# Fetching the last image's rows inside the loop of a two-layer convolution and state-space kernel

## The chip, the cores and the metric

The kernel runs on one core of a Trainium2 chip. The metric is the device time of one execution in microseconds, as the median of several runs; for the kernel before it is 13595.54 us (three runs, 13595.24 to 13596.91). The engines are called PE (matrix products), ACT (activations), DVE (vector work), POOL (GpSimd) and SP, which does no arithmetic here and issues nearly all transfers between main memory and the on-chip buffers.

## The reference

Eight images of 128 channels by 128 by 128 pass through two layers. The first (a dilated convolution, Fourier transforms and an attention over channels) is not touched. The second is, cut to what matters:

```python
y = conv2d(x, conv_w, 3x3, padding 1) + conv_b
seq = y.reshape(B * H * W, 8, 16)          # 8 tokens of 16 channels in each pixel
xi, z = split(seq @ in_proj)
xc = silu(causal_conv1d(xi)); dt, B, C = split(xc @ x_proj)
dt = softplus(dt * dt_w + dt_b)
for t in range(8):                          # 32 x 16 states in each pixel
    h = exp(dt[t] * A) * h + dt[t] * B[t] * xc[t]
    y[t] = sum(h * C[t])
out = ((y + D * xc) * silu(z)) @ out_proj
g = (out - mean) / sqrt(var + eps)          # in 4 groups of channels, over the whole image
return x + silu(g * gn_w + gn_b)
```

The mean and variance run over an image, so the last line can be computed for an image only when all of its rows are through.

## The kernel before, in words

Layer 2 (`layer1` in the code) cuts each image into 32 blocks of four rows (`RB = 4`), 256 blocks in all, `nb = 256`. All engines follow one order written out by hand: the tuple `ORDER` lists the pieces of work of one turn of the loop, each with a number `ahead`; in turn `i` a piece works on block `i + ahead`. So a turn holds the end of block `i - 1`, the middle of block `i` and the beginning of blocks `i + 1` and `i + 2`. Each engine runs its instructions strictly in this order, and SP issues its transfers in it too.

What the pieces around the change do, with the lines of the profile:

- `exps` (ACT, L851), `decay` (DVE, L870, L873, L875), `inject` (DVE L864, two of 16 on POOL L862), `add` (DVE, L880) and `weigh` (POOL, L886) are the scan over tokens, in 16 steps `s` a block. A step's state lies in a buffer `h` (`hp`, nine of them, 128 x 1024 values of four bytes), its weighted state in a buffer `hc` (`hcp`, nine). `collect` (PE, L987) and `ends_sum` (PE, L952, L957) sum the `hc` into the block's output and so free them. The first two steps of `weigh` in POOL's turn are 8 and 15; `decay` of step 15 multiplies what `weigh` of step 15 made.
- `lay_first` and `lay_ends` (SP, L913 and L905/L906) put rows of two projections into `bcs`; `end_products` (POOL, L935) multiplies them to `cb`, the first thing POOL does in a turn; `lay_cross` (SP, L943) spreads `cb` to `cbx`, which `cross` (DVE, L892) uses.
- `store_inputs` and `lay_inputs` (SP, L824, L831) pass `u` through main memory to `ud` for POOL's `inject`; `lay_states` (SP, L815) spreads the projections to `bb` and `cc`.
- `lay_own` and `lay_own_first` (SP, L924, L930) gather rows of `u` into `us`; `own_terms` (DVE, L964) multiplies them with what `ends_sum` made; `own_add` (PE, L971), `gated` (DVE, L994), `project_out` (PE, L1002), `result` (ACT, L1012) and `spread_of` (ACT, L1020/L1021) follow it, and `keep` (SP, L1025) stores the block's output to `gn` in main memory.
- `norm` calls `norm_of` (L1036 to L1055) when an image's last block is through: from the sums it makes a scale `sc` and an offset `bi`.

The last line of the reference is done for image 0 to 6 inside the loop, one block of rows a turn, while the next image is under way: `last_load` (SP, L1070/L1071, two loads of 256 KB into `v` and `res`, two buffers each), `last_act` (ACT, L1077, a Silu, with a load of ACT's function table before it and one for the exponential after it), `last_sum` (POOL, L1083) and `last_store` (SP, L1089). Since the seventh image's norm comes in turn 226, two of its 32 blocks of rows are left when the loop ends; a small loop does them there.

For the last image nothing is under way any more. Its 128 rows are done in 16 groups of eight rows (`TR = 8`), `k = 0 .. 15`: `tail_load(k)` takes one of the nine `h` and one of the nine `hc` buffers and loads 512 KB of `gn` (SP, L1133) and 512 KB of `x1` (SP, L1134) into them; `tail(k)` does the Silu (ACT, L1139), the sum (DVE, L1140) and the store of 512 KB (SP, L1141). Six groups are loaded ahead (`AHEAD = 6`).

SP has eight semaphores for its transfers and takes them in turn, so a transfer is issued only when the one eight before it has landed.

Of the kernel before, what the change touches and what calls it, by code (L numbers as in the profile page):

```python
# [595 lines left out]
def layer1(ctx, tc, x1, w1, c1, out):  # L596
# [96 lines left out]
    nb = len(blocks)  # L693
# [10 lines left out]
    def live(i):  # L704
        return 0 <= i < nb
# [321 lines left out]
    def norm_of(b):  # L1027

        mv = wk2.tile([P, 2], F32, name="mv")
        gmv = wk2.tile([P, 2], F32, name="gmv")  # L1030
        dv = wk2.tile([P, 1], F32, name="dv")
        sc = wk2.tile([P, 1], F32, name="sc")
        bi = wk2.tile([P, 1], F32, name="bi")
        nr = H // RB
        st, dm = stats[b], wk1.tile([P, nr], F32, name="dm")
        nc.vector.tensor_reduce(mv[:, 0:1], st[:, 0], AX.X, ALU.add)  # L1036
        nc.vector.tensor_scalar(mv[:, 0:1], mv[:, 0:1], 1.0 / HW, None, ALU.mult)
        nc.vector.tensor_scalar(dm, st[:, 0], 1.0 / N, mv[:, 0:1], ALU.mult, ALU.subtract)
        nc.vector.tensor_mul(dm, dm, dm)
        nc.vector.scalar_tensor_tensor(dm, dm, float(N), st[:, 1], ALU.mult, ALU.add)  # L1040
        nc.vector.tensor_reduce(mv[:, 1:2], dm, AX.X, ALU.add)
        nc.vector.tensor_scalar(mv[:, 1:2], mv[:, 1:2], 1.0 / HW, None, ALU.mult)
        ps = misc().rearrange("p a b -> p (a b)")
        nc.tensor.matmul(ps[:, 0:2], cf("group"), mv, start=True, stop=True)
        nc.vector.tensor_copy(gmv, ps[:, 0:2])
        nc.vector.tensor_sub(dv, mv[:, 0:1], gmv[:, 0:1])
        nc.vector.tensor_mul(dv, dv, dv)
        ps = misc().rearrange("p a b -> p (a b)")
        nc.tensor.matmul(ps[:, 0:1], cf("group"), dv, start=True, stop=True)
        nc.vector.tensor_scalar(sc, ps[:, 0:1], gmv[:, 1:2], GN_EPS, ALU.add, ALU.add)  # L1050
        nc.scalar.activation(sc, sc, AF.Sqrt)  # L1051
        nc.vector.reciprocal(sc, sc)  # L1052
        nc.vector.tensor_mul(sc, sc, wf("gn_w"))  # L1053
        nc.vector.tensor_mul(bi, gmv[:, 0:1], sc)  # L1054
        nc.vector.tensor_sub(bi, wf("gn_b"), bi)  # L1055
        tails.extend((b, r, sc, bi) for r in range(0, H, RB))
# [6 lines left out]
    loaded, active, summed = [], [], []  # L1063

    def last_load(i):
        if tails:
            b, r, sc, bi = tails.pop(0)
            v = wk2.tile([P, RB, W], F32, name="v")
            res = wk2.tile([P, RB, W], F32, name="res")
            nc.sync.dma_start(v, gns[b][:, r:r + RB, :])  # L1070
            nc.sync.dma_start(res, x1[b][:, r:r + RB, :])  # L1071
            loaded.append((b, r, sc, bi, v, res))

    def last_act(i):
        if loaded:
            b, r, sc, bi, v, res = loaded.pop(0)
            nc.scalar.activation(v, v, AF.Silu, bias=bi, scale=sc)  # L1077
            active.append((b, r, v, res))

    def last_sum(i):  # L1080
        if active:
            b, r, v, res = active.pop(0)
            nc.gpsimd.tensor_add(res, res, v)  # L1083
            summed.append((b, r, res))

    def last_store(i):
        if summed:
            b, r, res = summed.pop(0)
            nc.sync.dma_start(out[b, :, r:r + RB, :], res)  # L1089
# [38 lines left out]
    def tail_load(k):  # L1128
        if k < len(ends_of):
            b, r = ends_of[k]  # L1130
            v = hp.tile([P, TR, W], F32, name="h")
            res = hcp.tile([P, TR, W], F32, name="hc")
            nc.sync.dma_start(v, gns[b][:, r:r + TR, :])  # L1133
            nc.sync.dma_start(res, x1[b][:, r:r + TR, :])  # L1134
            held[k] = v, res

    def tail(k, sc, bi):
        (b, r), (v, res) = ends_of[k], held.pop(k)
        nc.scalar.activation(v, v, AF.Silu, bias=bi, scale=sc)  # L1139
        nc.vector.tensor_add(res, res, v)  # L1140
        nc.sync.dma_start(out[b, :, r:r + TR, :], res)  # L1141

    AHEAD = 6
    E = mybir.EngineType
    with tc.manual_schedule(engines={E.PE, E.Activation, E.DVE, E.Pool, E.SP}):
        for i in range(-4, nb + 3):
            for f, ahead, *k in ORDER:
                if live(i + ahead) or i + ahead == -1 and f in FIRST:
                    f(i + ahead, *k)
        i = nb  # L1150
        while tails or loaded or active or summed:
            last_load(i)
            last_act(i)
            last_sum(i)
            last_store(i)
        assert not tails
        for k in range(AHEAD):
            tail_load(k)
        b = ends_of[0][0]
        norm_of(b)  # L1160
        _, _, sc, bi = tails[0]
        for k in range(len(ends_of)):
            tail(k, sc, bi)
            tail_load(k + AHEAD)


def network(tc, x, w0, w1, c0, c1, out):
    B = x.shape[0]
    with tc.tile_pool(name="dram", bufs=1, space=DRAM) as dram:
        x1 = [dram.tile([C, H, W], F32, name=f"x1_{b}") for b in range(B)]  # L1170
        layer0(tc, x, w0, c0, x1)
        layer1(tc, x1, w1, c1, out)
# [73 lines left out]
```

## Time and profile before

| what | us |
|---|---|
| median of the runs | 13595.54 |
| profiled execution, its own time | 13597.71 |
| profiled execution, span | 13594.9 |
| busy: PE, DVE, POOL, ACT | 13227.2, 11943.4, 11940.1, 10091.1 |
| one block in the loop | 44.5 |
| end of the last matrix product of `project_out`, from the span's start | 13517.13 |
| first load of the last image's rows | 13529.72 |
| first store of the last image's rows | 13539.48 |

All times of events are counted from the span's start in the one profiled execution. "A <- B" behind an idle time names what ended it. A time of an SP line is that of issuing a transfer, not of its landing; the landing is in a view of its own. Busy times of PE are of pipelined work and say little alone.

### The profile page before, as it was taken

To read this page: it belongs to the slowest core of one execution; us is meant where nothing else is said; L and a number is where in the kernel's file an instruction comes from. 1 tells how busy PE (TensorE), PEld (TensorE's weight loads), DVE (VectorE), ACT (ScalarE), POOL (GpSimd) and SP (SyncE) were. 2 spreads that over 40 slices of the span, in tenths; PEclk is the share of its full clock that TensorE was granted. 3 is DMA by queue.
4 is the path that set the end of the run, shared out by engine and by line. 5 is a ranking of instruction groups with operands and counts; after the bars stand their busy time and mean duration, and the time that the engine had idled before them with its cause. 6 is when DMAs were issued, how large, how long until landed. Compare 5 with 4: busy or idle time off the path is not lost. (4 is left out here: it accounts for less than half of the span.)

```text
span 13594.9 us, 255193 instructions
## 1 busy us (share of the span) xinstructions
PE 13227.2 (97%) x97850; PEld 4812.6 (35%) x97850; DVE 11943.4 (88%) x11710; ACT 10091.1 (74%) x11827; POOL 11940.1 (88%) x6533
## 2 busy tenths in 40 slices
PE   9999999999999999999999999999999999999996
PEld 5676663333333333332333333332333333323332
DVE  3343349999999999999999999999999999999997
ACT  3454367777788878887888878887888788878886
POOL 6766659999899999999999989999999999989996
PEclk9999999999999999999999999999999999999998
DMA  4544455555566666666666666666666666666666
GB/s 132 160 133 125 144 128 135 134 129 135 137 154 149 152 145 153 152 150 147 150 154 150 149 146 151 153 149 148 148 154 152 144 153 150 154 142 154 150 150 177
DMA packets 1183640, 1996.65 MB, mean 147 GB/s; under 512 B 149616, under 2 KB 411824, under 8 KB 1174224
## 3 DMA queue, kind: packets, MB, share of 16 engines
q1 hardware_dynamic: 1181840, 1977.82, 60.0%
q8 instruction: 769, 12.60, 0.4%
q14 instruction: 455, 3.73, 0.1%
q10 hardware_dynamic: 576, 2.50, 0.1%
HBM read 687.75 MB, written 218.10 MB: 67 GB/s over the span
## 5 line engine op out<-in xcount | busy, mean ns | idle before, releaser
L886 POOL TENSOR_TENSOR hc<-h,cc 128x1024 f32<-128x1024 f32 x3584 | 8424.7, 2375 | 308.2 <-PE s L840 219.9
L851 ACT ACTIVATE s<-s 128x1024 f32<-128x1024 f32 x3584 | 3558.2, 1005 | 1185.5 <-PE s L840 1166.7
L840 PE MATMUL s<-dt,m_a 32*128 32x512 f32 x14336 | 3525.2, 638 | 17.0 <-DVE h L880 14.5
L875 DVE TENSOR_TENSOR s<-s,h 128x1024 f32<-128x1024 f32 x2560 | 3134.3, 1224 | 46.0 <-ACT s L851 22.4
L864 DVE TENSOR_TENSOR h<-s,bb 128x1024 f32<-128x1024 f32 x2560 | 3100.6, 1215 | 55.2 <-DMA bb<-all_b 20.2
L880 DVE TENSOR_TENSOR h<-s,h 128x1024 f32<-128x1024 f32 x2560 | 3094.7, 1217 | 54.5 <-DVE s L875 1.8
L840 PE MATMUL s<-u,l_ct 32*128 32x512 f32 x10240 | 2892.2, 641 | 50.2 <-DVE h L873 18.4
L734 PE MATMUL pm<-xin,l_wt 128*32 128x508 f32 (+3 forms) x18432 | 2409.2, 595 | 6.2 <-DVE wk L650 5.5
L987 PE MATMUL yps<-hc,l_ct 128*32 128x512 f32 x14336 | 1889.6, 598 | 61.5 <-ACT yps L980 55.9
L851 ACT ACT_TABLE_LOAD x1247 | 1599.9, 1283 | 235.8 <-DVE h L880 136.6
L840 PEld LDWEIGHTS s<-dt,m_a 32*128 32x128 f32 x14336 | 969.1, 183 | 1275.0 <-DVE h L880 629.7
L840 PEld LDWEIGHTS s<-u,l_ct 32*128 32x128 f32 x10240 | 768.2, 183 | 1438.5 <-DVE h L880 521.2
L862 POOL TENSOR_TENSOR h<-ud,bb 128x1024 f32<-128x1024 f32 x512 | 1220.8, 2384 | 2.4 <-DMA ud<-uw 2.4
L792 POOL TENSOR_TENSOR u<-dt,xc 128x512 f32<-128x512 f32 x512 | 656.0, 1281 | 458.5 <-ACT dt L787 456.6
L734 PEld LDWEIGHTS pm<-xin,l_wt 128*32 128x32 f32 x18432 | 469.3, 109 | 1588.4 <-issue 1586.7
L987 PEld LDWEIGHTS yps<-hc,l_ct 128*32 128x32 f32 x14336 | 394.9, 109 | 1288.8 <-issue 1024.3
L870 DVE TENSOR_TENSOR hc<-s,hc 128x1024 f32<-128x1024 f32 x512 | 623.6, 1218 | 199.4 <-ACT s L851 191.0
L787 ACT ACT_TABLE_LOAD x511 | 655.6, 1283 | 40.9 <-PE pm L782 23.9
L980 ACT ACTIVATE yps<-xc,l_wt 128x512 f32<-128x512 f32 x511 | 352.1, 689 | 403.3 <-DVE ym L994 403.3
L873 DVE TENSOR_TENSOR h<-s,h 128x1024 f32<-128x1024 f32 x512 | 621.5, 1214 | 0.0
L892 DVE TENSOR_TENSOR hc<-s,cbx 128x1024 f32<-128x1024 f32 x512 | 620.4, 1212 | 0.0
L782 PE MATMUL pm<-xc,m_dt 128*32 128x512 f32 x4096 | 545.6, 605 | 1.4 <-ACT yT L752 0.7
(202 smaller groups left out, 15362.6 us busy)
## 6 DMA issues: line engine op xcount, KB each, us to landing
cc<-all_c SPq DMA_DIRECT2D x1792, 256.0 KB, 5.5
bb<-all_b SPq DMA_DIRECT2D x1536, 256.0 KB, 5.7
ud<-uw SPq DMA_DIRECT2D x1024, 256.0 KB, 4.1
xin<-x SPq DMA_DIRECT2D x152, 768.0 KB, 5.1
xin<-x SPq DMA_DIRECT2D x112, 640.0 KB, 6.6
us<-u SPq DMA_DIRECT2D x1025, 64.0 KB, 1.9
cbx<-cb SPq DMA_DIRECT2D x512, 128.0 KB, 2.4
gn<-xr SPq DMA_DIRECT2D x256, 256.0 KB, 2.2
```

Source lines behind the costliest of these rows:

```text
L734: nc.tensor.matmul(d["pm"][c, a:b, wa:wb], convw[:, t, c], xin[:, r + dy + a - lo:r + dy + b - lo, wa + dx:wb + dx], start=(k == 0), stop= ...
L787: nc.scalar.activation(d["dt", hf], flat(d["pm"]), AF.Softplus, bias=wf("dt_b"))
L792: nc.gpsimd.tensor_mul(d["u", hf], d["dt", hf], d["xc"][:, hf, :])
L840: nc.tensor.matmul(d[name, s][:, q], m[a:a + DI, t % LP, :], d[src, t // LP][a:a + DI, :], start=True, stop=True)
L851: nc.scalar.activation(da, da, AF.Exp)
L862: nc.gpsimd.tensor_mul(h, d["ud", t][:, k:k + GP, :], state_row(i, "bb", t))
L864: nc.vector.tensor_mul(h, d["ups", s], state_row(i, "bb", t))
L870: nc.vector.tensor_mul(d["hc", s], da, d["hc", s])
L875: nc.vector.tensor_mul(da, da, d["h", s - GP])
L880: nc.vector.tensor_add(h, d["da", s], h)
L886: nc.gpsimd.tensor_mul(hc, d["h", s if t < L - 1 else s - GP], state_row(i, "cc", t))
L987: nc.tensor.matmul(d["yps"][g * DI:(g + 1) * DI], gather[:, t % LP, :], d["hc", GP * t + g // GP][:, g % GP], start=False, stop=t in LAST, ...
```

## The change

Two things change, both in the part of `layer1` that runs the order.

First, in the last four turns that work on a block `i` (252 to 255), the pieces of the last line are run a second time at the end of the turn: what is loaded, computed or summed is carried through to its store (`last_act`, `last_sum`, `last_store` until nothing is left), and then one more group of rows is loaded with `last_load`. So a turn does two of the seventh image's blocks of rows instead of one. By the end of turn 254 all are loaded, and turn 255 stores the last.

Second, the first loads of the last image are no longer issued after the norm's predecessors at the end, but inside the loop, in turn 256, behind the last piece that takes an `h` or `hc` buffer (that is the `weigh` of step 12 of block 255), and they are nine groups instead of six. The later ones are issued, as before, one after each `tail(k)`, now for group `k + 9`.

```diff
-    AHEAD = 6
+    AHEAD = 9
+    TAKES = (inject, decay, weigh, cross)
+    last_i = nb - 1 - min(ahead for f, ahead, *_ in ORDER if f in TAKES)
+    last_at = max(at for at, (f, ahead, *_) in enumerate(ORDER) if f in TAKES and last_i + ahead == nb - 1)
+    MORE = 4
     E = mybir.EngineType
     with tc.manual_schedule(engines={E.PE, E.Activation, E.DVE, E.Pool, E.SP}):
         for i in range(-4, nb + 3):
-            for f, ahead, *k in ORDER:
+            more = nb - MORE <= i < nb
+            for at, (f, ahead, *k) in enumerate(ORDER):
                 if live(i + ahead) or i + ahead == -1 and f in FIRST:
                     f(i + ahead, *k)
+                if (i, at) == (last_i, last_at):
+                    for k in range(AHEAD):
+                        tail_load(k)
+            if more:
+                while loaded or active or summed:
+                    last_act(i)
+                    last_sum(i)
+                    last_store(i)
+                last_load(i)
         i = nb
         while tails or loaded or active or summed:
             last_load(i)
...
         assert not tails
-        for k in range(AHEAD):
-            tail_load(k)
         b = ends_of[0][0]
         norm_of(b)
```

In the built order `keep` of block 254 and `lay_own_first` of block 255 stand on SP behind the eighteen loads, since they come later in `ORDER`. At the ends of turns 252, 253 and 254 SP has, ahead of the next turn's transfers, two stores (L1089) and two loads (L1070, L1071); POOL has one more L1083 behind its last `weigh` of the turn and ahead of `cb`; ACT has one more L1077 with its table load, and one more table load for L851.

## Prediction

> **What bounds the kernel now.** I read first the busy times by stretch, one block (44.5 us) to a line, then what DVE and POOL waited for, then the timeline of one block boundary, then the timeline of the end with the DMA issues.
>
> ```profile
> 13308.00:13352.50 44.50, 44.20 (x340) 13.74 (x340) 43.33 (x40) 36.20 (x41) 41.84 (x21) 1.00 0.62 145
> 12134.50:12179.00 44.50, 35.39 (x240) 11.16 (x241) 39.26 (x43) 28.16 (x32) 29.52 (x14) 0.85 0.47 119
> 13530.00:13595.00 65.00, 0.00 (x0) 0.00 (x0) 19.82 (x18) 21.11 (x17) 0.00 (x0) 0.50 0.99 391
> ```
>
> ```profile
> DVE hc L870 <- ACT s L851: 178.8, 235, 1.1
> ...
> POOL cb L935 <- DMA bcs<-all_c: 98.2, 91, 2.6
> ```
>
> Columns of the first three: stretch, its length, then PE, PEld, DVE, ACT, POOL, granted clock, DMA share, GB/s. A usual block is bound by DVE: its one regular wait is 0.75 us, before `decay` of step 15 (L870), so whatever stops DVE longer is lost. The second line is a block in which PE sat idle for 8.04 us (an image's norm): the clock fell to 0.85. The third is the end: DMA 0.99, nothing else busy for a third of it. The waits (total us, times, longest) say that POOL's `cb` (L935) is already held at times by rows (`bcs`) that SP lays.
>
> The boundary between blocks 253 and 254 (start, duration, engine):
>
> ```profile
> 13392.99 0.60 SPq L913 DMA_DIRECT2D bcs<-all_b  x1
> 13393.68 0.60 SPq L913 DMA_DIRECT2D bcs<-all_c  x1
> ...
> 13394.74 2.36 POOL L886 TENSOR_TENSOR hc<-h,cc 128x1024 f32<-128x1024 f32 x1 [0.86 <-PE s L840]
> 13397.05 0.74 POOL L935 TENSOR_TENSOR cb<-bcs 128x256 f32<-128x256 f32 x1
> 13397.74 2.37 POOL L886 TENSOR_TENSOR hc<-h,cc 128x1024 f32<-128x1024 f32 x1
> 13400.48 7.00 POOL L886 TENSOR_TENSOR hc<-h,cc 128x1024 f32<-128x1024 f32 x3 [0.37 <-DVE h L873]
> ...
> 13404.01 1.23 DVE L870 TENSOR_TENSOR hc<-s,hc 128x1024 f32<-128x1024 f32 x1 [0.76 <-ACT s L851]
> ```
>
> SP lays `bcs` before POOL has finished the old block; then `cb`, `weigh` 8, `weigh` 15, and L870 takes what `weigh` 15 made.
>
> The end:
>
> ```profile
> 13512.03 0.69 DVE L964 TENSOR_TENSOR own<-pm,us 128x512 f32<-128x512 f32 x1 [5.62 <-PE yps L987]
> ...
> 13529.72 0.42 SPq L1133 DMA_DIRECT2D h<-gn  x1
> 13530.10 0.16 DVE L1055 TENSOR_TENSOR bi<-l_wt,bi 128x1 f32<-128x1 f32 x1
> ...
> 13539.48 0.34 SPq L1141 DMA_DIRECT2D out<-hc  x1
> ```
>
> ```profile
> out<-res SPq DMA_DIRECT2D x2, 256.0 KB, 2.2
> h<-gn SPq DMA_DIRECT2D x16, 512.0 KB, 10.0
> ```
>
> `own_terms` of block 255 (L964) starts the chain to the norm's `bi`; the first of 16 stores leaves at 13539.48, the span ends at 13594.9. A load of 512 KB lands 4.06 us after its issue when first (13529.72, its ACT_TABLE_LOAD starts at 13533.78), 10.0 us in a full queue; there one transfer takes 1.28 us (first ACTIVATEs on new `h` at 13536.89, 13539.45, 13542.03: 2.56 for two).
>
> **What the skill says.** "DMA: Bandwidth & Descriptors", Queues, rings and completion order: SP has one row of rings, and a ring's descriptors are consumed in order. The trace agrees: 512 KB takes 10 us with eight transfers outstanding, about 8 x 1.28. "TensorE: Matmul & The Clock Gate", HAM oscillation: PE gaps over some 3.4 us halve the clock; here 8.04 us did (0.85 over that block). "ScalarE: Activation LUTs", What ACT_TABLE_LOAD costs: 1283 ns and a drain of 1380 ns. The trace shows the 1.28 and no drain (the ACTIVATE follows 0.01 us later); I take 1.28.
>
> **The change, part by part.** The sum is against the profiled execution: span 13594.9, 13597.71 in all, 2.2 over the median.
>
> (a) Second leftover at the ends of blocks 252, 253, 254. ACT gets, after `result` (ends 13396.48), a table load, a Silu and a table load back: 1.28 + 0.81 + 1.28 = 3.37. `exps` 10 then ends at 13400.9 instead of 13397.8; DVE loses 2.85 there. The Silu ends at 13398.6, so POOL's new sum runs 13398.65 to 13399.93. SP waits for it: its new store stands *ahead* of the next block's issues. Behind it wait one `v` and one `res` load, `uw`, both `bcs`, `us`, `cbx`, `ud`, `bb`, `cc`. From 13399.95: store 0.45, `v` 0.6, `res` 0.45, `uw` 0.8, first `bcs` 0.65, so the second is issued at 13402.9 and lands about 2.3 later (the tile's landings: 1.9 least, 2.0 median), 13405.2. Only then runs `cb`: to 13406.0; `weigh` 8 to 13408.3; `weigh` 15 to 13410.65. L870 starts there instead of 13404.01: 6.64 lost, the 2.85 within it. Later users have room: `ud` lands by 13414 for an `inject` at 13423; `bb` by 13417 for DVE at 13422. POOL, 8.0 late, catches up in its 2.7 us of idle time per block. Three boundaries: 19.9. PE sits idle some 4 us at each. Where the norm halved the clock, DVE waited 1.67 and 0.69 more; I take about 1 a boundary (bounds 0 and 2.4): 3. Sum of (a): **+23**.
>
> (b) Leftovers gone from the end. They delayed the square root: `sc` is there at 13521.81, and without them `bi` is done 1.05 later, at 13522.85 instead of 13530.26: **-7.4**.
>
> (c) Nine pairs of loads after the last `weigh` in SP's order. Each waits for its `hc` buffer, freed in PE's order: after `collect` of 8 (13502.3), of 10 (13504.8), of 11 (13509.3), the two `cross` (13510 to 13511), the last four (to 13513.7). Behind all eighteen stand `keep` of block 254 and the last row of `us` (lay_own_first, L930; issued at 13494.75 now), and `own_terms` waits for that row. From the third `hc` on, the bytes queue: first landing 13509.35 + 4.06 = 13513.4, the second 1.75 later as in the present burst, then eleven more at 1.28 to 13529.3; `keep` and `us` 0.9: 13530.2. SP may have eight outstanding, so it can't even issue `us` before the eighth transfer ahead of it has landed (13521.6). `own_terms` starts at 13530.2 instead of 13512.03: +18.2; its chain runs at half clock after that PE gap, +0.9 (16 matmuls of L1002 take 2.00 at full clock): **+19.1**. Bounds: if `us` overtakes the loads in 1.9 us, +11.6; if they are slower, +21.
>
> (d) The tail. From `bi` to the first store 1.28 + 1.24 + 1.22 and gaps = 3.8. Nine tiles lie ready; 16 stores and 7 pairs are left, 30 transfers where 48 were. But with nine buffers, and all nine in use, the `hc` load of tile k+9 waits for store k to *land*, and store k+1 stands behind that load on SP. So seven turns are a chain, not a stream. In a turn the load and the next store are issued within 0.8 us of a landing, the store behind the load. No row shows it. Below: bytes alone, 3 x 1.28 = 3.84. Above: the present burst's pair, second landing 4.06 + 1.76 = 5.8. A 256 KB store alone lands after 2.2 against 2.9 for a load, so a store second comes sooner: I take 5.0. First store landed after 3.0, six turns 30, last load and nine stores 4.06 + 9 x 1.28 = 15.6, end of program 1.6: 50.2. With 3.8: 54.0 from `bi`, where it is 64.6 now (13594.9 - 13530.26): **-10.6** (-19 to -5).
>
> Sum: 23 - 7.4 + 19.1 - 10.6 = **+24.1 us**. On the median, 13595.5 + 24.1 = 13620, slower by 0.18%.
>
> What can be told from no change is put at 0.2%, 27.2 us, so this stands just inside it.
>
> **Rivals.**
> 1. *Slower by more than that.* Same mechanism, with the clock: each PE gap halves it for several windows and DVE waits 2.4 a boundary (+4), a turn costs 5.8 (+5.6): +34, 13629. For: block 254 has no convolutions and shows 2.17 us of such a wait already. Against: at the norm most of the half clock cost nothing. It decides from 3 us above my sum.
> 2. *Not slower.* One mechanism: the boundary stall is absorbed. Stretches 13444 to 13492 and later have DVE at 42.85 of 48.0, so a late start might only fill idle time; (a) falls to 0 and +1 is left, -7 if the turns run at the byte rate: 13588 to 13597. Against: in 252 and 253 DVE has 0.75 us of idle time, and POOL, PE and ACT shift with it. It decides where L870 starts less than 0.5 us late.
> 3. *The row of `us` is not held*, landing 1.9 after issue: (c) falls by 7.5, +17, 13612. Against: the order of the ring.
> 4. *The change does not fetch early*: no. In the built order the loads stand in block 256, ahead of the norm, each waiting for its own buffer alone.
>
> **How the numbers follow.** The forecast, +24 with some 6 us either way, 0.48, of which 0.12 lies over 27.2; rival 1, +27 to +45, 0.30; rival 3, 0.11; rival 2, 0.08; a gain over 27.2, 0.03: (a) at nothing, `us` free and turns at the byte rate together give only 24 - 23 - 7.5 - 8.1 = -15, so it would need something I don't see. Slower 0.12 + 0.30 = 0.42, within 0.2% 0.36 + 0.11 + 0.08 = 0.55, faster 0.03. The likeliest is the sum, 13620. Range: down to rival 3's 13612 with a few us of (d), 13604; up past rival 1, 13636.
>
> **What would show it.** Right: at three boundaries SP's second L1089 after POOL's second L1083, `cb` waiting for `bcs` by 5 us, L870 waiting for POOL about 5 us; L964 waiting 17 us for a DMA of `us` late in the end; PE idle beside a full DMA; in the tail SP's L1134 waiting for `out<-hc`, stores 5 us apart, then 1.28. Wrong: `cb` on time, L964 released by PE, or stores 3.8 apart from the first.

## The result and the profile after

The changed kernel takes 13625.08 us (median of 14 runs, 13621.84 to 13631.74), the kernel before in the same session 13596.2 (14 runs, 13593.6 to 13598.76). The ratio is 1.0021 with a 95% interval of 1.0013 to 1.0029: slower by 28.9 us, where +24.1 was forecast. The profiled span is 13624.4 where it was 13594.9, 29.5 more.

The table divides the 29.5 by stage. A stage ends where one instruction starts in both profiles: `decay` 15 (L870) of each turn, then `own_terms` of block 255 (the last L964), then the norm's `bi` ready (start of the last L1055 plus its 0.16), then the end of the span.

| stage | before, us | after, us | difference | forecast |
|---|---|---|---|---|
| up to L870 of turn 252, ahead of the change | 13315.03 | 13318.28 | +3.3 | 0 |
| L870 of turn 252 to 253 | 44.49 | 50.79 | +6.3 | |
| 253 to 254 | 44.49 | 50.64 | +6.2 | |
| 254 to 255 | 47.0 | 54.34 | +7.3 | |
| 255 to 256 | 48.96 | 47.87 | -1.1 | |
| the four together, (a) | 184.94 | 203.64 | +18.7 | +23 |
| L870 of turn 256 to `own_terms`, (c) | 12.06 | 31.32 | +19.3 | +18.2 |
| `own_terms` to `bi`, (b) and the half clock of (c) | 18.23 | 12.43 | -5.8 | -7.4 + 0.9 |
| `bi` to the end, (d) | 64.64 | 58.73 | -5.9 | -10.6 |

The +3.3 of the first row arises before anything of the change has run. Over the profiles of this study that L870 starts anywhere from 13311.31 to 13322.88, so the row says how far two profiles differ by themselves; the stages below it give +26.3.

The boundary between blocks 253 and 254, POOL's timeline of the kernel after (start, duration, engine; the bracket holds the idle time before and what ended it):

```profile
13404.30 2.36 POOL L886 TENSOR_TENSOR hc<-h,cc 128x1024 f32<-128x1024 f32 x1 [0.90 <-DMA bb<-all_b]
13408.24 1.26 POOL L1083 TENSOR_TENSOR res<-res,v 128x512 f32<-128x512 f32 x1 [1.59 <-ACT v L1077]
13414.33 0.72 POOL L935 TENSOR_TENSOR cb<-bcs 128x256 f32<-128x256 f32 x1 [4.83 <-DMA bcs<-all_c]
13415.01 9.28 POOL L886 TENSOR_TENSOR hc<-h,cc 128x1024 f32<-128x1024 f32 x4
```

SP's timeline of the same boundary, and after it SP's issues at the end of the kernel:

```profile
13399.69 10.18 SPq L1089 DMA_DIRECT2D out<-res  x2
13409.93 0.42 SPq L1070 DMA_DIRECT2D v<-gn  x1
13410.44 0.40 SPq L1071 DMA_DIRECT2D res<-x  x1
13410.90 0.51 SPq L824 DMA_DIRECT2D uw<-u  x1
13411.46 0.61 SPq L913 DMA_DIRECT2D bcs<-all_b  x1
13412.17 0.60 SPq L913 DMA_DIRECT2D bcs<-all_c  x1
...
13516.68 0.54 SPq L1133 DMA_DIRECT2D h<-gn  x1
...
13542.16 0.32 SPq L1134 DMA_DIRECT2D hc<-x  x1
13543.45 0.32 SPq L1025 DMA_DIRECT2D gn<-xr  x1
13544.68 0.51 SPq L930 DMA_DIRECT2D us<-u  x1
```

The first line holds both stores of the turn: SP stands in it for 10.18 us, until POOL's second sum ends at 13409.50. Only then come the five issues down to `bcs`, the last at 13412.17. In POOL's view `cb` waits 4.83 us for it, where it followed its predecessor at once before, and the first two `weigh` behind it (merged into the x4) bring L870 to 13419.71. At the end the same shape returns: `us` (L930) stands behind all eighteen loads, the last issued at 13542.16.

What DVE waited for from 13340 on (total us, times, longest), then PE's timeline at two boundaries:

```profile
DVE hc L1140 <- DMA hc<-x: 26.5, 6, 4.7
DVE own L964 <- DMA us<-u: 25.1, 1, 25.1
DVE hc L870 <- POOL hc L886: 11.3, 4, 4.1
DVE s L875 <- ACT s L851: 10.7, 7, 2.8
```

```profile
13362.13 1.13 PE L840 MATMUL s<-u,l_ct 32*128 32x512 f32 x4 [2.55 <-DVE h L873]
...
13412.93 2.07 PE L840 MATMUL s<-u,l_ct 32*128 32x512 f32 x4 [4.05 <-DVE h L873]
```

The third and fourth waits are for the most part the two halves of a boundary: ACT late by 2.8 us (`exps` behind the Silu and the tables), then POOL late by up to 4.1. In PE's view the same four products take 1.13 us after a gap of 2.55 and 2.07 after 4.05, so the clock is halved at once at the second boundary. At the first it falls too, only a little later. A stretch behind it (columns as in the prediction; the clock is the 0.50):

```profile
13364.00:13367.00 3.00, 3.00 (x16) 0.60 (x16) 0.94 (x1) 2.78 (x4) 3.00 (x3) 0.50 0.47 117
```

At the second boundary the half clock shows from 13412.93 on, less than 7 us before the L870 that ends the step. So what it costs has to be looked for in the next step too: 253 to 254 has a mean clock of 0.93, and 254 to 255, the one of +7.3, has 0.80.

The end, from the chain of waits (start, length, what was waited for or run):

```profile
13533.50 11.17 DMA hc<-x
13544.68 8.43 DMA us<-u
13553.24 0.70 DVE own L964
...
13572.88 6.09 DMA out<-hc
13578.98 0.32 SPq L1134
13579.40 5.39 DMA out<-hc
13584.80 0.32 SPq L1134
13585.22 5.34 DMA out<-hc
```

The eighth semaphore back (a load of `hc`, 11.17 us) holds the issue of `us`; its 64 KB then take 8.43 us to land, where the median landing of that row is 1.9. The tail below is a chain of one thing: a store lands, SP issues the `hc` load that waited for its buffer, and 0.42 us after the landing the next store. One turn is 0.42 + 5.4 = 5.8 us.

Lengths, busy times (PE, PEld, DVE, ACT, POOL), clock, DMA share and GB/s of two stretches of the kernel after:

```profile
13404.00:13455.00 51.00, 41.08 (x236) 12.36 (x239) 40.55 (x38) 35.08 (x39) 39.79 (x20) 0.80 0.55 131
...
13578.00:13624.40 46.40, 0.00 (x0) 0.00 (x0) 9.15 (x8) 7.90 (x7) 0.00 (x0) 0.50 0.84 289
```

The first is the block behind the second boundary: DVE works 40.55 of 51 us where a usual block has 43.3 of 44.5. The second is the tail: the transfers move 289 GB/s, where the kernel before had 391 in its own.

### The profile page after: what moved, and what is told of

Its sections match the earlier page's. It is cut to its first block, busy times and chain, and to the rows that moved or that the text cites. A ratio compares the mean times of both kernels' runs of the same rounds, so it can differ in the third digit from the quotient of the medians.

```text
span 13624.4 us, 255211 instructions
## 1 busy us (share of the span) xinstructions
PE 13235.4 (97%) x97850; PEld 4814.3 (35%) x97850; DVE 11947.4 (88%) x11710; ACT 10099.1 (74%) x11832; POOL 11939.8 (88%) x6533
## 5 line engine op out<-in xcount | busy, mean ns | idle before, releaser
L851 ACT ACTIVATE s<-s 128x1024 f32<-128x1024 f32 x3584 | 3558.4, 1005 | 1184.9 <-PE s L840 1166.2
L870 DVE TENSOR_TENSOR hc<-s,hc 128x1024 f32<-128x1024 f32 x512 | 624.5, 1220 | 209.7 <-ACT s L851 185.8
L971 PE MATMUL yps<-own,l_ct 128*32 128x512 f32 x4096 | 534.0, 593 | 20.3 <-DVE own L964 20.3
```

The source lines that it names most:

```text
L851: nc.scalar.activation(da, da, AF.Exp)
L870: nc.vector.tensor_mul(d["hc", s], da, d["hc", s])
```

## The experiments

The theory is that of the prediction; each experiment undoes one part or does one part alone, and the last puts together what was learnt. Lines of a diff are against the changed kernel unless said otherwise. "Before" is always the kernel before, run in the same session: 13597.12 us (57 runs) for the first four, 13596.08 (49 runs) for the others.

**Each part alone.** First the loads inside the loop without the second leftover a turn, then the second leftover with the loads at the end again.

```diff
-    MORE = 4
+    MORE = 0
```

> The change without its second leftover in turns 252 to 254 (the loads of the last image stay inside the loop). My theory, with the stage times of the two profiles: the three block boundaries lose nothing (-18.7 against the changed kernel), the two leftovers come back before the norm (+5.8 to +7.4), own_terms of block 255 still waits about 25 us for the row of us and the tail still turns in 5.7 us. So 12 us under the changed kernel, 13613, which is still 13 to 17 over the kernel before. Rival (the fetch is a gain and the leftovers alone are the loss): below the kernel before, 13580 to 13590.

Measured: 13612.01, ratio 1.0011 (1.0005 to 1.0018), +14.9. The four steps of L870 sum to 183.0 us (before 184.9); L870 to `own_terms` takes 30.0; the tail's stores are about 6 us apart.

```diff
-    AHEAD = 9
+    AHEAD = 6
...
-                if (i, at) == (last_i, last_at):
-                    for k in range(AHEAD):
-                        tail_load(k)
...
         assert not tails
+        for k in range(AHEAD):
+            tail_load(k)
```

> The second leftover alone; the last image is loaded after the loop, six groups ahead, as before. My theory: three boundaries of 6 us or more, 18.7 in all, less the 5.8 to 7.4 that the leftovers cost at the end: 11 to 13 over the kernel before, 13608; POOL's cb waits some 5 us for bcs at three boundaries, own_terms does not wait for a DMA. Rival (the fetch is the loss, the boundaries are hidden): 13589, 7 under the kernel before.

Measured: 13606.92, ratio 1.0006 (0.9998 to 1.0015), +9.8; the interval reaches over no change. The steps sum to 202.9, `own_terms` is released by PE 12.16 us after L870, and `bi` follows 10.78 us later.

What follows: the boundary stall belongs to the leftovers and the 19 us before `own_terms` to the loads, each in its own stage. The two medians add to +24.7, beside +28.9 for the whole change. One gain is counted twice in that sum: with the leftovers gone and the loads still at the end, the first load leaves 6.32 us after `own_terms` instead of 17.69, and from it to the end both kernels take 65.2. So the leftovers are worth 11.4 us there, 3.9 more than what reaches `bi`, while in the whole change the loads are early already.

PE's timeline of the second kernel at its first boundary, and the stretch behind it:

```profile
13364.65 2.08 PE L840 MATMUL s<-u,l_ct 32*128 32x512 f32 x4 [2.55 <-DVE h L873]
```

```profile
13364.50:13370.50 6.00, 5.85 (x24) 1.94 (x28) 3.05 (x4) 4.82 (x5) 4.34 (x3) 0.50 0.47 137
```

The gap is the 2.55 us of the changed kernel, but here the clock is down at once, and for 6.8 us instead of 3.4. The step takes 50.75 us, in the changed kernel 50.79: at this boundary the half clock costs nothing that shows.

DVE's timelines of the two kernels, at `own_terms`:

```profile
13529.24 0.69 DVE L964 TENSOR_TENSOR own<-pm,us 128x512 f32<-128x512 f32 x1 [23.42 <-DMA out<-res]
```

```profile
13535.80 0.69 DVE L964 TENSOR_TENSOR own<-pm,us 128x512 f32<-128x512 f32 x1 [5.62 <-PE yps L987]
```

In the first, 23.42 us of waiting are put down to another transfer (`out<-res`), a store that `own_terms` doesn't use. That is the case in which the last event isn't the cause; the test of the cause is the next kernel.

**The row of `us` ahead of the loads.** The eighteen loads move to just behind `keep` of block 254 and `lay_own_first` of block 255.

```diff
-    last_at = max(at for at, (f, ahead, *_) in enumerate(ORDER) if f in TAKES and last_i + ahead == nb - 1)
+    last_at = max(at for at, (f, ahead, *_) in enumerate(ORDER) if f is lay_own_first)
```

> The changed kernel with the eighteen loads put behind keep of block 254 and lay_own_first of block 255 in SP's order. My theory: own_terms of block 255 is released by PE again, about 12 us after decay of step 15 instead of 31: -19.3 against the changed kernel, of which up to 4 come back because the loads then still run when the first stores leave: 13606 to 13610. The tail's turns stay at 5.7 us. Rival (own_terms is late because memory is full, not because of the order in SP's queue): own_terms waits for the row as long as in the changed kernel, 13625.

Measured: 13607.24, ratio 1.0008 (1.0000 to 1.0016), +10.1. From DVE's and from SP's timeline:

```profile
13529.36 0.69 DVE L964 TENSOR_TENSOR own<-pm,us 128x512 f32<-128x512 f32 x1 [5.62 <-PE yps L987]
```

```profile
13544.03 0.34 SPq L1141 DMA_DIRECT2D out<-hc  x1
13544.47 0.45 SPq L1133 DMA_DIRECT2D h<-gn  x1
13548.89 0.32 SPq L1134 DMA_DIRECT2D hc<-x  x1
13549.30 0.38 SPq L1141 DMA_DIRECT2D out<-hc  x1
```

L870 to `own_terms` is 12.17 again: the whole +19.3 was two transfers standing behind the loads, and the wait for PE is the 5.62 of the kernel before. The last of the loads is issued 19.7 us after L870 (20.2 in the changed kernel), so they are as early as they were. In SP's lines the `hc` load follows the landing of the store of 13544.03, at 13548.89, and the next store comes right behind it: the stores are still 5.3 to 5.9 us apart, and the tail takes 60.05 us from `bi`.

**SP's order at the boundary.** ACT's Silu and POOL's sum stay where the change puts them; the second store and the two loads move behind `lay_cross` of the next turn.

```diff
+                if f is lay_cross and nb - MORE < i <= nb:
+                    while summed:
+                        last_store(i)
+                    last_load(i)
...
-                while loaded or active or summed:
+                while loaded or active:
                     last_act(i)
                     last_sum(i)
-                    last_store(i)
-                last_load(i)
```

> The changed kernel with SP's part of the second leftover (its store and the next v and res load) moved behind lay_cross of the next turn; the Silu on ACT and the sum on POOL stay at the end of the turn. My theory (SP held by the store delays bcs and so cb): cb is on time after the sum, the step from one decay 15 to the next grows by 2.8 to 3.3 us a boundary (ACT's 3.37) instead of 6.3, so -9 to -10 against the changed kernel, 13615. Rival (ACT's and POOL's extra work is itself the price): 6 us a boundary as before, 13625.

Measured: 13618.35, ratio 1.0016 (1.0009 to 1.0022), +21.2. The steps are 48.22, 48.52, 49.87 and 48.75. POOL's timeline:

```profile
13407.42 1.26 POOL L1083 TENSOR_TENSOR res<-res,v 128x512 f32<-128x512 f32 x1 [1.58 <-ACT v L1077]
13408.63 0.72 POOL L935 TENSOR_TENSOR cb<-bcs 128x256 f32<-128x256 f32 x1
```

`cb` waits for nothing any more. The four steps fall from 203.6 to 195.4, by 8.3; 10.4 over the kernel before remain, 3.7, 4.0 and 2.9 at the three boundaries, where 2.8 to 3.3 each were expected. The 8.3 is the upper end: over the five profiles that have the leftovers as in the change the steps sum to 202.1 to 203.6.

**Without the Silu of the second leftover.** The kernel just shown, with one thing more: the activation of the second leftover, and so the two table loads around it, is left out in 3 of the 256 blocks of rows; the sum adds the values without it. The lines are against that kernel.

```diff
-                while loaded or active:
-                    last_act(i)
+                while loaded:
+                    b, r, sc, bi, v, res = loaded.pop(0)
+                    active.append((b, r, v, res))
+                while active:
```

> The run with SP's part later, and without the Silu of the second leftover in turns 252 to 254 (its sum takes v as loaded; three of 256 blocks of rows lack their normalisation). My theory (what was left of the boundary's price, 2.9 to 4.0 us each, is ACT's two table loads and Silu ahead of the exponentials): the step from one decay 15 to the next is back at 44.5 to 45.8, POOL's 1.28 for the sum hidden in its idle time. Rival (POOL's sum ahead of cb is the price): steps stay at 48.2 to 48.5.

Measured: 13604.39 (one run), steps 44.5, 44.49, 46.54 and 48.57, in sum 184.1. POOL's timeline:

```profile
13398.68 1.29 POOL L1083 TENSOR_TENSOR res<-res,v 128x512 f32<-128x512 f32 x1
13399.91 0.74 POOL L935 TENSOR_TENSOR cb<-bcs 128x256 f32<-128x256 f32 x1
```

POOL's 1.29 us sum is still there, and the first two blocks take 44.5 us again, so that sum was free. With the two together the +18.7 divides into 8.3 for SP's order (203.6 to 195.4), 11.3 for ACT's work and what comes with it, PE's gap among it (195.4 to 184.1), and -0.8 for the rest (184.1 against 184.9), which is no more than profiles differ: those of the four kernels without the stop sum to 183.0 to 185.8.

**The tail's turns.** Two ways of breaking the chain. The first keeps nine groups, with `us` ahead of the loads, and refills three groups later, so that SP issues a load for a buffer whose store is long on its way.

```diff
-            tail_load(k + AHEAD)
+            if k >= 3:
+                tail_load(k - 3 + AHEAD)
```

> As the run with us first, and in the tail the loads of group k + 9 are issued after group k + 3 instead of after group k, so that the store whose buffer they take has landed by then. My theory (in the tail SP stands at each hc load until the store just issued has landed): the turns of 5.3 to 5.8 us go, the tail runs at the byte rate of 1.28 us a transfer: 12 us less than with us first alone, 13594 to 13596, about the time of the kernel before. Rival (the turns are slow because loads and stores share memory): the same as with us first alone, 13607.

Measured: 13593.07, ratio 0.9998 (0.9989 to 1.0006), -3.0; the interval reaches over no change. The stores, from SP's timeline:

```profile
13563.43 0.34 SPq L1141 DMA_DIRECT2D out<-hc  x1
13564.62 0.32 SPq L1133 DMA_DIRECT2D h<-gn  x1
13565.87 0.32 SPq L1134 DMA_DIRECT2D hc<-x  x1
13567.18 0.34 SPq L1141 DMA_DIRECT2D out<-hc  x1
```

They are 3.75 us apart, the issues even at 1.2 to 1.3 us, and `bi` to the end takes 47.33 us instead of 60.05.

The second changes one number of the changed kernel: eight groups ahead, with nine buffers, so a load always finds one that isn't the one just being stored.

```diff
-    AHEAD = 9
+    AHEAD = 8
```

> The changed kernel with AHEAD = 8: one pair of buffers stays free, so the load of group k + 8 waits for the store of group k - 1 instead of that of group k. My theory (with all nine pairs taken, the load waits for the store just issued): turns of about 4 us instead of 5.7, and us lands two transfers (2.6 us) earlier: 12 under the changed kernel, 13613. Rival (fewer groups ready at the norm is what counts): 2.6 slower for the two transfers more that are left, 13626.

Measured: 13615.01, ratio 1.0012 (1.0006 to 1.0019), +18.9. From `bi` to the end it is 48.85 us instead of 58.73, and from the fourth on the turns take 3.75 to 3.79 us. From SP's timeline:

```profile
13578.83 0.32 SPq L1134 DMA_DIRECT2D hc<-x  x1
13579.24 0.41 SPq L1141 DMA_DIRECT2D out<-hc  x1
13579.74 0.46 SPq L1133 DMA_DIRECT2D h<-gn  x1
13582.61 0.32 SPq L1134 DMA_DIRECT2D hc<-x  x1
```

All three transfers of a turn are still issued within 1 us, as in the changed kernel. So it is not the bunching that makes a turn slow, but waiting for the store just issued: here the `hc` load waits for the store before that one, and a turn more is under way. The wait for `us` stays (22.71 us).

**A version from what was learnt.** The loads stand behind `us`; the refills lag; no leftover is doubled. What is left of the seventh image after its block of turn 256, its last eight rows, becomes the first group of the tail, worked on behind `own_terms` of block 255, so its store leaves before `bi` is known. The lines are against the kernel before; the nine groups and the place of the loads are as above.

```diff
-    ends_of = [(nb // (H // RB) - 1, r) for r in range(0, H, TR)]
+    ends_of = [(B - 2, H - TR)] + [(B - 1, r) for r in range(0, H, TR)]
...
+                if i == nb and f is own_terms:
+                    (_, _, sc, bi), _ = tails
+                    tails.clear()
+                    tail(0, sc, bi)
+        assert not (tails or loaded or active or summed)
+        tail_load(AHEAD)
+        norm_of(B - 1)
...
-        for k in range(len(ends_of)):
+        for k in range(1, len(ends_of)):
             tail(k, sc, bi)
-            tail_load(k + AHEAD)
+            if k >= 3:
+                tail_load(k - 2 + AHEAD)
```

> No second leftover in the loop; the seventh image's last two blocks are done as one group of eight rows in an h and an hc buffer, loaded first, its Silu and sum in turn 256 beside own_terms; the loads stand behind us; reloads lag. My theory: no boundary cost, own_terms and bi on time without the leftovers (bi at about 13523 of the span), the tail at the byte rate: 51 transfers from about 13511 on at 1.28 us, 4 of them done: 13574 to 13580, some 20 under the kernel before. Rival (the fetch inside the loop costs as much as it gives): 13595.

Measured: 13578.45, ratio 0.9988 (0.9981 to 0.9994): 17.6 us faster than the kernel before. From its DVE timeline:

```profile
13509.78 0.69 DVE L964 TENSOR_TENSOR own<-pm,us 128x512 f32<-128x512 f32 x1 [6.49 <-PE yps L987]
...
13520.55 0.16 DVE L1055 TENSOR_TENSOR bi<-l_wt,bi 128x1 f32<-128x1 f32 x1
```

Against the kernel before, by the stages of the table: the steps +0.9, L870 to `own_terms` +0.6, `own_terms` to `bi` -7.3, `bi` to the end -12.75 (51.89). The gain is in the last two; what each of the three mends gives to it was not measured one by one.

## Why the prediction came out right

All four mechanisms held. The sum came near, +24.1 for +28.9, partly by luck: (a) was put 4.3 us too dear and the gain of (d) 4.7 too large, and the two cancel. Nor did the likelier outcome come: the prediction gave 0.55 to a change within 27.2 us and 0.42 to a slower kernel, and +28.9 lies just past that line, with an interval that covers both sides of it.

- **(a), the boundaries.** The stop of L870, forecast at 6.64 a boundary, was 6.3, 6.2 and 7.3: 19.8 in sum for 19.9. The path is the one written down, SP's store behind POOL's sum, `bcs` late, `cb` late. Moving only SP's transfers took 8.3 us of it away, and the Silu the rest. That the 2.85 of ACT lie within the 6.64 is right for the kernel as it is; it also means that mending SP's order alone leaves a boundary late by 2.9 to 4.0. The term that was mis-sized is the 3 us for the halved clock, put on top of the stops: the three steps leave no room for it. The clock did halve at the boundaries, and after a shorter gap than the 4 us written down. The Trainium skill ("TensorE: Matmul & The Clock Gate", HAM oscillation) speaks of gaps of PE over some 3.4 us; here 2.55 were enough, and the measurement decides. In the first two steps the half clock costs nothing that shows: over the five profiles with these leftovers they lie between 50.6 and 50.8 us at mean clocks of 0.93 to 0.97. For the third step, block 254 without convolutions, it stays open. The four kernels without the stop take 45.9 us at a mean of 0.94, 46.5 at 0.93, 47.0 at 0.91 and 48.3 at 0.82, so there a longer step goes with a lower clock; but two kernels with the stop, both at 0.80, take 52.2 and 54.3. The fourth step came out 1.1 shorter than before, which was not foreseen; over all ten profiles it lies between 47.5 and 49.0, so this may be no more than spread.
- **(b), the leftovers gone.** -5.8 for -6.5 (with the 0.9 of the half clock). With `us` ahead of the loads, or the loads at the end, the stage takes 10.8, 7.4 less than before: the -7.4 was exact, and the half clock behind the wait for `us` cost 1.6 instead of 0.9. There PE is on the chain: the last fourteen products of L1002 take 3.25 us, at a clock of 0.50, and 1.77 with `us` ahead of the loads.
- **(c), `us` behind the loads.** 19.3 for 18.2, the largest term measured and the best one. The eight semaphores show: 13544.68 is the moment when the eighth transfer back lands. The Trainium skill ("DMA: Bandwidth & Descriptors", Queues, rings and completion order) says that a ring's descriptors are consumed in order, and the trace agrees: ahead of `us` six loads of 512 KB and the 256 KB of `keep` are still under way, by estimate 6 x 1.28 + 0.64 = 8.3 us, and the row lands after 8.43. Rival 3, in which the row isn't held, is out, since moving two transfers took the whole 19 away.
- **(d), the tail.** -5.9 for -10.6. The chain was right, the turn wrong: 5.0 was taken, 5.7 to 6.5 were measured. It rested on the step that "a store second comes sooner". It does not come sooner: in the chain a store lands 5.25 to 5.5 us after its issue (the first one 6.09), and with the 0.42 between the landing and that issue the turn is 5.8, what the prediction had as its upper bound, the second landing of two loads (4.06 + 1.76). The six turns between the first landing and the last load took 35.5 us instead of 30; what follows them came 0.8 shorter.

Of the rivals, the first (slower by more) was to decide from 3 us above the sum, and the medians are 4.8 above it. It has its turn of 5.8; its 2.4 us of clock a boundary are not in the first two steps. The second, with the stall absorbed, is out: with the leftovers alone the steps are as long as in the changed kernel. About 3 us of the profiled difference lie ahead of the change; whether any of them is its own stays open, as it is no more than profiles differ in that place.

Not tried: whether the loads would stand in nobody's way if another engine than SP issued them.

## What to carry to other kernels

A transfer that is put early into an engine's issue order is paid for by everything it is put ahead of: read the issue order behind the new place, look for the smallest row there that someone waits for, and put that first. Where transfers refill the buffers they have just emptied, keep one buffer or more between the refill and the store; using all of them "to load more ahead" turns a stream (3.75 us a turn here) into a chain (5.8). And a piece doubled to fill idle engines is priced by what stands behind it in each queue: here POOL's 1.26 us were free, ACT's 3.4 us and SP's place in the order were not.

## What the runs showed of the hardware

- A small transfer behind large ones is slow twice: the 64 KB row was issued only when the eighth transfer back had landed, and then took 8.43 us, where the median of that row is 1.9.
- A turn of three transfers of 512 KB takes 5.8 us when its load waits for the store just issued, and 3.75 to 3.79 when it waits for the store before that, though in both the three are issued within 1 us. 3.75 is about the rate of the bytes (3 x 1.28 = 3.84 by the kernel before).
- A gap of 2.55 us on PE was followed by a halved TensorE clock for 3.4 us in the changed kernel and for 6.8 with the leftovers alone. Both steps took 50.8 us: there, where DVE waits for POOL, it cost nothing that shows. With PE on the chain, behind the wait for `us`, it cost 1.6 us.
